# A two-layer graph network on one core: a re-planned instruction order, PSUM banks named by the planner, and layer norms' reciprocal roots on ScalarE

## The chip, the core and the metric

The kernel runs on one core of one Trainium2 chip. The metric is the device time in microseconds of one execution. Before the change it was 4487.69 us, the median of three runs (4481.99, 4487.69, 4490.15).

## The reference, cut to what matters

The input `x` is 16 batches of 1024 rows by 256 columns in fp32; `adj` is 16 matrices of 1024 by 1024 int32, of which only "larger than zero" matters. Two layers follow each other for each batch by itself.

Layer 0 is graph attention with 8 heads of width 32, and is followed by a layer norm, a product, a second layer norm and a residual:

```
q, k, v = heads(x @ Wq), heads(x @ Wk), heads(x @ Wv)
e = q k^T;  e = where(e >= 0, e, 0.2 * e)
h = softmax(where(adj > 0, e, -9e15)) @ v
x1 = layernorm(concat(layernorm(h), x) @ Wffn.T) + x
```

Layer 1 runs two more attentions whose scores are only a sum of a row term and a column term, then two layer norms around a feed-forward net of width 1024:

```
gat(h): Wh = h @ W; e = leaky_relu(Wh @ a_left + (Wh @ a_right)^T)
        softmax(where(adj > 0, e, -9e15), over rows) @ Wh
h = layernorm(x1 + gat(gat(x1)))
out = layernorm(h + relu(h @ w_ff1 + b_ff1) @ w_ff2 + b_ff2)
```

A layer norm multiplies each row by rsqrt(var + 1e-5). With four layer norms to a batch this reciprocal root of a column of variances is wanted in 14 places a batch, 224 in all.

## The kernel before, in words

**Engines.** TensorE does all products and transposes. For one head and one block of 128 keys (a "step", 1024 of them in all) TensorE makes 128x1024 scores (L601, tile `ps_s`), ScalarE multiplies them by 0.2 (L619), VectorE takes the larger of the two (L621), ScalarE takes the exponential (L624), GpSimd multiplies by the mask (L628), and TensorE multiplies by the values (L650, tile `ps_a`, two halves of the array at once with 33 or 64 columns each). The rest of a batch goes through tiles of one PSUM bank called `ps_m`: transposes of `x` (L355) and of the mask (L422), projections of q and k (L475, their high and low halves taken out in L478 on ScalarE and L480 on VectorE) and of v (L507), the head outputs (L677), the product with Wffn (L753, L756), layer 1's products (L785, L876, L901), and the feed-forward net (L941, L969, with L929 adding the residual). Each such tile is emptied by ScalarE or VectorE. The weights of layer 1's attention are made by VectorE alone (`attend`, L838 and L841).

**The order is written out by a planner.** All work is in Python generators ("threads"). Before anything is issued, a thread says `yield on(ENGINE=cost)`; it takes buffers by `yield take(pool)`, gives them back by `yield give(pool)`, and waits for events of other threads. The class `Order` keeps a clock for each engine and steps from one operation to the next: among those that could begin within 300 ns (`WINDOW`) of the earliest one it takes the one with the smallest due time (`aim`). The order in which the planner releases the threads is the program's order on each engine's queue; on the chip each engine works through its queue in that order and waits by semaphores. So the costs given to `on` and the constants `HOP` (added after each operation before another engine may go on) have no effect on what is computed. They set the order alone. Due times come from two tables of shares of a batch's slot of 253 us: `EARLY` for the first two batches, `AIM` for all the others and for the paces of the first, second and last batch (`fast0`, `fast1`, `fast15`).

**Buffers.** PSUM has 8 banks: two `scores` tiles of two banks each, one `acc` bank for the values, and three `misc` banks. `misc()` asks a pool with `bufs=3` for a tile, and the framework picks one of the three; the planner's own pool only counts them. `p` has five buffers.

**Around the change.** From the second batch on, `all_scores` takes both score buffers and issues the scores of two steps at once (`n = 2`). `all_values` waits for two steps (`GV = 2`) and issues both as one operation of the planner, cost `240 + 860 * GV`, and gives both `p` buffers back after it. `stats` computes mean and variance on VectorE (L333, L335), and then on GpSimd adds epsilon (L338) and raises to the power -0.5 (L340); `normalized` (L349) and the feed-forward's end (L982) wait for it. The GpSimd queue holds the 1024 mask products L628, and these 448 small instructions between them.

Batches overlap: while the scores of batch b are made, the rest of batch b-1 and the projections of batch b+1 fill TensorE's queue.

Of the kernel before, what the change touches and what calls it, by code (L numbers as in the profile page):

```python
# [18 lines left out]
EPS = 1e-5  # L19
# [15 lines left out]
class Order:  # L35
# [5 lines left out]

    HOP = dict(PE=100.0, ACT=70.0, DVE=60.0, POOL=70.0, SP=60.0)
    WINDOW = 300.0

# [3 lines left out]
    def __init__(self, **pools):  # L54
        self.clock = defaultdict(float)
        self.port = 0.0
        self.transfers = 0.0
        self.stretch, self.done, self.half = 0, 0.0, True
        self.pools = {k: [0.0] * n for k, n in pools.items()}
        self.queues = defaultdict(list)  # L60
        self.events = {}
        self.waiting = defaultdict(list)
        self.active = []
        self.made = 0
        self.now = 0.0
        self.busy = defaultdict(float)

    def add(self, thread, aim, ready=0.0):
        self.made += 1
        self.step({"gen": thread, "aim": aim, "no": self.made, "ready": ready}, None)  # L70

    def step(self, th, sent):
        while True:
# [19 lines left out]
            elif what == "take":  # L93
# [3 lines left out]
                th["ready"] = max(th["ready"], self.pools[arg].pop(0))  # L97
            elif what == "give":
                queue = self.queues[arg]
                if queue:  # L100
                    other = min(queue, key=lambda o: (o["aim"], o["no"]))
                    queue.remove(other)
                    other["ready"] = max(other["ready"], th["ready"])
                    self.step(other, None)
                else:
                    self.pools[arg].append(th["ready"])
# [27 lines left out]
    def run(self):  # L134
        while self.active:
            could = []
            for th in self.active:
                costs, shared, delay = th["op"]
                best = None
                for engine, cost in costs.items():  # L140
                    ready = th["ready"]
                    if th.get("last", ())[:2] == (engine, ready):
                        ready -= self.HOP[engine]
                    t = max(self.clock[engine], ready)
                    if shared and engine in ("DVE", "POOL"):
                        t = max(t, self.port)
                    if best is None or t + cost < best[0] + best[2]:
                        best = t, engine, cost
                could.append((best, th))
            first = min(c[0][0] for c in could)  # L150
            (t, engine, cost), th = min((c for c in could if c[0][0] <= first + self.WINDOW),
                                        key=lambda c: (c[1]["aim"], c[1]["no"]))
            if th["op"][1] and engine in ("DVE", "POOL"):

                lead = 100.0 if engine == "DVE" else -100.0
                before = [c for c in could if c[1]["op"][1] and c[0][1] in ("DVE", "POOL")
                          and c[0][1] != engine and c[0][0] + lead < t]
                if before:
                    (t, engine, cost), th = min(before, key=lambda c: (c[1]["aim"], c[1]["no"]))
            costs, shared, delay = th["op"]  # L160
            self.active.remove(th)
            end = self.clock[engine] = self.end(engine, t, cost)
# [4 lines left out]
            th["ready"] = end + self.HOP[engine]  # L167
# [10 lines left out]
def on(shared=False, delay=0.0, **costs):  # L178
    return "on", (costs, shared, delay)
# [45 lines left out]
def unshifted_path(  # L225
# [28 lines left out]
    AIM = dict(mask0=0.759, x=0.818, x_step=0, mask=0.747, mask_step=0.0264, qk0=0.614, qk1=0.898,  # L254
               qk_step=0.0231, v0=0.832, v1=0.974, v_step=0.0591, rows=-0.244, rows_step=0.0408, first0=0.12,
               first1=0.252, graph0=-0.009, graph1=0.21, graph_step=0, second=0.355, second_step=0.0335,
               normed=0.78, normed_step=0.026, ff_wait=(None, 0, 1, 0), ff=(0.532, -0.011, 0.487, 0.497),
               ff_step=0.0386, fast0=0.425, fast1=0.938, fast15=0.832, lead=3.15)

    EARLY = dict(x=0.87, x_step=0.005, mask=0.747, mask_step=0.0296, qk0=0.692, qk1=0.909, qk_step=0.0345,  # L260
                 v0=0.774, v1=1.001, v_step=0.0568, rows=-0.139, rows_step=0.0071, first0=0.082, first1=-0.169,
                 graph0=-0.195, graph1=-0.027, graph_step=0, second=0.302, second_step=0.0335, normed=0.781,
                 normed_step=0.02, ff_wait=(None, 0, 1, 0), ff=(0.633, -0.001, 0.488, 0.497), ff_step=0.0386)
# [13 lines left out]
    def misc(dtype=FT):  # L277
        return psum.tile([P, HALF], dtype, tag="misc", name="ps_m", bufs=bufs["misc"])
# [9 lines left out]
    minus_half = const.tile([P, TPH], FT, name="minus_half")  # L288
    nc.gpsimd.memset(minus_half, -0.5)
# [25 lines left out]
    def evacuate(n):  # L315
        return on(DVE=140 + 1.06 * n, ACT=150 + 0.87 * n)

    def evacuate_by(n):

        return on(DVE=190 + 1.06 * n, ACT=250 + 0.87 * n)  # L320
# [5 lines left out]
    def stats(srcs):  # L326
# [3 lines left out]
        for i, src in enumerate(srcs):  # L330
            st = small.tile([P, 6], FT, name="st")
            yield on(DVE=420)
            nc.vector.bn_stats(st, src)  # L333
            yield on(DVE=185)
            nc.vector.bn_aggr(mv[:, i, :], st)  # L335
        rs = small.tile([P, n], FT, name=f"rs{n}")
        yield on(POOL=260)
        nc.gpsimd.tensor_scalar(rs, mv[:, :, 1], EPS, None, op0=OP.add)  # L338
        yield on(POOL=450 + 150 * n, shared=True)
        nc.gpsimd.tensor_tensor(rs, rs, minus_half[:, :n], op=OP.pow)  # L340
        return mv, rs

    def normalized(dst, srcs, mv, rs):
        for i, (row, src) in enumerate(zip(dst, srcs)):
            if row is src:
                yield on(DVE=340, shared=True)
            else:
                yield on(DVE=440)
# [38 lines left out]
    def mask_part(b, t, halves):  # L387
# [22 lines left out]
        for i, ai in enumerate(ints):  # L410
            yield on(DVE=440, shared=True)
# [8 lines left out]
        yield on(PE=90 + 112 * n)  # L420
# [3 lines left out]
        yield on(ACT=150 + 225 * n)  # L424
# [19 lines left out]
    def x_pair(b, u):  # L444
# [7 lines left out]
        yield on(PE=450)  # L452
# [7 lines left out]
    def qk_part(b, g, o, nh):  # L460
# [12 lines left out]
        yield on(PE=1720)  # L473
# [3 lines left out]
        yield on(ACT=590)  # L477
        nc.scalar.copy(high.bitcast(FR), pa)  # L478
        yield on(DVE=690)
# [20 lines left out]
    def v_part(b, g, u):  # L500
# [3 lines left out]
        yield on(PE=1000)  # L504
# [15 lines left out]
    def project_v(b, g, t0):  # L520
# [3 lines left out]
        yield on(POOL=500)  # L524
# [5 lines left out]
    def warm_up():  # L530
# [3 lines left out]
        nc.scalar.copy(small.tile([P, TPH], FT, name="warm", bufs=1), minus_half)  # L534
# [46 lines left out]
    def all_scores():  # L581
        for b in range(B):
# [4 lines left out]
            for h in range(H):  # L587
                yield wait(("stack", b, h))
                q, kk = stacks[b, h]
                n = 2 if b else 1  # L590
                for t in range(0, NT, n):
                    due = t0 + (h * NT + t) / 2 * pace(b)
                    yield aim(due, AIM["lead"] * PACE)
                    for _ in range(n):
                        yield take("scores")
                    ps = [psum.tile([P, N], FT, tag="scores", name="ps_s") for _ in range(n)]
                    yield on(PE=450 * n)
                    for i in range(n):
                        for nh in range(NH):
                            cols = slice(nh * HALF, (nh + 1) * HALF)  # L600
                            nc.tensor.matmul(ps[i][:, cols], kk[:, (t + i) * P:(t + i + 1) * P], q[:, cols],  # L601
                                             start=True, stop=True)
                    if t + n == NT:
                        yield give("stacks")
                    for i in range(n):
                        yield start(weights(b, h, t + i, ps[i]), due + i * PACE / 2)

    def weights(b, h, t, ps):
# [3 lines left out]
        if b == 0:  # L612
            engine = yield on(ACT=1050, DVE=1230)
        else:
            engine = yield on(ACT=1050)
# [4 lines left out]
        yield on(DVE=1220)  # L620
        nc.vector.tensor_tensor(p, p, ps, op=OP.max)  # L621
        yield give("scores")
        yield on(ACT=1080)
# [3 lines left out]
        yield on(POOL=2050, shared=True)  # L627
# [3 lines left out]
    def all_values():  # L631
        for b in range(B):
            for h in range(H):
# [6 lines left out]
                for d in range(0, NT, GV):  # L640
                    for t in range(d, d + GV):
                        yield wait(("p", b, h, t))
                    yield aim(begin[b] + (h * NT + d + 2) / 2 * pace(b), SLOT)
                    yield on(PE=240 + 860 * GV)
                    for t in range(d, d + GV):
                        p = probs.pop((b, h, t))
                        for nh in range(NH):

                            m = VW if t else 64
# [796 lines left out]
```

## Time and profile before

| what | us |
|---|---|
| runs | 4481.99, 4487.69, 4490.15 |
| span of the profiled execution, first to last instruction | 4479.9 |
| TensorE busy with matmuls | 4325.9 (97%) |
| VectorE busy | 3311.9 (74%) |
| ScalarE busy | 2887.7 (64%) |
| GpSimd busy | 2474.9 (55%) |
| mean granted TensorE clock | 0.990 |

The profile gives a span for the profiled execution and no other time of it; the three runs lie 2.1 to 10.2 us above that span, the median 7.8 us. An engine's idle time says what it waited for last. TensorE's matmuls are pipelined, so a short wait can hide under the draining end of the matmul before it and then counts as busy; distances from one start to the next show it.

### The profile page before, as it was taken

The numbers are of one execution on the slowest core, as the hardware profiler recorded it, in microseconds if no ns is written. First come the engines' busy times: TensorE is split into PE (matmuls) and PEld (weight loads), VectorE is DVE, ScalarE is ACT, GpSimd is POOL, SyncE is SP. The second block draws the span as 40 slices with busy tenths as digits, with TensorE's granted clock in tenths as the row PEclk, the third lists the DMA queues.
The fourth block names the chain that finished last, engine by engine and source line by source line (L and its number), as shares of the span: only waits on it lengthen the run. The fifth ranks groups of instructions, "written<-read, shape, count | busy, mean of one in ns | idle before, by whom it ended". The sixth has DMA issues, their size and how long they took to land.

```text
span 4479.9 us, 57088 instructions
## 1 busy us (share of the span) xinstructions
PE 4325.9 (97%) x20299; PEld 2866.3 (64%) x20299; DVE 3311.9 (74%) x5263; ACT 2887.7 (64%) x4015; POOL 2474.9 (55%) x1544
## 2 busy tenths in 40 slices
PE   8888999999999999999999999999999999999998
PEld 3444656667666675766667666676666667666587
DVE  6877867687776877778777776877778777776754
ACT  6666675666667666666666666666666666666631
POOL 5756565554565556556554565546556554665610
PEclk9989999999999999999999999999999999999999
DMA  6423222232232313223231232323223231232100
GB/s 187 114 66 87 66 73 77 73 92 73 68 88 63 107 59 86 76 59 99 64 106 55 74 96 62 103 63 80 80 64 99 64 102 55 71 92 55 27 22 20
DMA packets 156209, 343.57 MB, mean 77 GB/s; under 512 B 21751, under 2 KB 24333, under 8 KB 155917
## 3 DMA queue, kind: packets, MB, share of 16 engines
q1 hardware_dynamic: 112140, 260.13, 20.8%
q10 hardware_dynamic: 43776, 79.71, 6.1%
q8 instruction: 164, 2.69, 0.3%
q14 instruction: 129, 1.05, 0.1%
HBM read 239.09 MB, written 100.66 MB: 76 GB/s over the span
## 4 chain that ended last, share of the span: by engine, by line
PE 69%; DVE 18%; issue 5%; POOL 5%; ACT 2%; DMA 0%; POOLq 0%; ACTq 0%; DVEq 0%
PE ps_a L650 16%; PE ps_s L601 9%; PE ps_m L901 8%; PE ps_m L876 8%; PE ps_m L941 7%; PE ps_m L969 6%; DVE att L841 5%; DVE att L838 5%; POOL p L628 4%; DVE p L621 4%; PE ps_m L785 3%; PE ps_m L475 3%; PE ps_m L753 2%; PE ps_m L756 2%; PE ps_m L355 2%
## 5 line engine op out<-in xcount | busy, mean ns | idle before, releaser
L628 POOL TENSOR_TENSOR p<-p,mask 128x1024 f32<-128x1024 f32 x1024 | 2232.2, 2197 | 1564.6 <-ACT p L624 1444.7
L621 DVE TENSOR_TENSOR p<-p,ps_s 128x1024 f32<-128x1024 f32 x1024 | 1211.1, 1214 | 399.3 <-ACT p L619 397.8
L624 ACT ACTIVATE p<-p 128x1024 f32<-128x1024 f32 x1024 | 1080.9, 1058 | 377.5 <-DVE p L621 355.7
L619 ACT ACTIVATE p<-ps_s 128x1024 f32<-128x1024 f32 x995 | 974.9, 1025 | 186.7 <-PE ps_s L601 172.1
L650 PE MATMUL ps_a<-p,v 128*33 128x512 f32 (+1 forms) x4096 | 1000.6, 606 | 24.2 <-POOL p L628 22.9
L601 PE MATMUL ps_s<-qs,ks 128*128 128x512 f32 x2048 | 634.5, 428 | 39.2 <-DVE p L621 38.3
L601 PEld LDWEIGHTS ps_s<-qs,ks 128*128 128x128 f32 x2048 | 349.5, 190 | 343.2 <-DVE p L621 106.2
L650 PEld LDWEIGHTS ps_a<-p,v 128*33 128x33 f32 (+1 forms) x4096 | 199.7, 114 | 531.3 <-issue 405.3
L901 PE MATMUL ps_m<-y,att 128*128 128x256 f32 x2048 | 480.5, 380 | 12.7 <-ACT v L516 11.0
L941 PE MATMUL ps_m<-rT,wf 128*128 128x256 f32 x2048 | 479.8, 384 | 10.7 <-ACT z L313 3.6
L969 PE MATMUL ps_m<-wf,hid 128*128 128x256 f32 x2048 | 475.1, 381 | 10.6 <-ACT xT L313 8.9
L876 PE MATMUL ps_m<-y,att 128*128 128x258 f32 x2048 | 472.4, 381 | 0.0
L969 PEld LDWEIGHTS ps_m<-wf,hid 128*128 128x128 f32 x2048 | 379.4, 190 | 78.6 <-issue 14.8
L876 PEld LDWEIGHTS ps_m<-y,att 128*128 128x128 f32 x2048 | 385.2, 189 | 63.6 <-issue 3.3
L901 PEld LDWEIGHTS ps_m<-y,att 128*128 128x128 f32 x2048 | 375.0, 189 | 77.3 <-ACT v L516 13.1
L941 PEld LDWEIGHTS ps_m<-rT,wf 128*128 128x128 f32 x2048 | 380.9, 192 | 63.4 <-ACT z L313 3.8
L838 DVE SCALAR_TENSOR_TENSOR att<-first,second 128x1024 f32<-128x1024 f32 x256 | 354.4, 1384 | 73.2 <-ACT first L825 73.2
L841 DVE SCALAR_TENSOR_TENSOR att<-mask,att 128x1024 f32<-128x1024 fp8e4 x256 | 352.0, 1375 | 8.7
L846 ACT ACTIVATE y<-y,check 128x258 f32<-128x258 f32 x256 | 130.9, 511 | 305.3 <-DVE check L844 278.4
L338 POOL TENSOR_SCALAR rs<-mv 128x2 f32<-128x2 f32 (+1 forms) x224 | 60.0, 268 | 410.9 <-DVE mv L335 410.8
L412 DVE TENSOR_SCALAR adj_b<-adj_i 128x512 fp8e4<-128x512 int32 x256 | 234.0, 958 | 14.8 <-DMA adj_i<-in_adj_dram 9.3
L950 ACT ACTIVATE hid<-ps_m,columns 128x256 f32<-128x256 f32 x372 | 159.2, 472 | 119.8 <-PE ps_m L941 94.3
(105 smaller groups left out, 4232.5 us busy)
## 6 DMA issues: line engine op xcount, KB each, us to landing
qs<-qk_halves SPq DMA_DIRECT2D x256, 256.0 KB, 4.2
ks<-qk_halves SPq DMA_DIRECT2D x256, 256.0 KB, 5.1
adj_i<-in_adj_dram ACTq DMA_DIRECT2D x240, 256.0 KB, 3.5
qk_halves<-high SPq DMA_DIRECT2D x128, 256.0 KB, 2.4
qk_halves<-low SPq DMA_DIRECT2D x128, 256.0 KB, 3.6
xr<-in_x_dram ACTq DMA_DIRECT2D x64, 256.0 KB, 3.1
x_kept<-x SPq DMA_DIRECT2D x64, 256.0 KB, 4.8
x<-x_kept SPq DMA_DIRECT2D x64, 256.0 KB, 6.8
```

The lines of the kernel that those rows point to most:

```text
L601: nc.tensor.matmul(ps[i][:, cols], kk[:, (t + i) * P:(t + i + 1) * P], q[:, cols], start=True, stop=True)
L619: nc.scalar.activation(p, ps, AF.Copy, scale=ALPHA)
L621: nc.vector.tensor_tensor(p, p, ps, op=OP.max)
L624: nc.scalar.activation(p, p, AF.Exp)
L628: nc.gpsimd.tensor_tensor(p, p, mask_of(b, t), op=OP.mult)
L650: nc.tensor.matmul(acc[nh * 64:nh * 64 + m, :], v[:, t, c:c + m], p[:, nh * HALF:(nh + 1) * HALF], start=(t == 0), stop=(t == NT - 1))
L838: nc.vector.scalar_tensor_tensor(e, first[:, 0, :], second[:, j:j + 1], first[:, 1, :], op0=OP.mult, op1=OP.max)
L841: nc.vector.scalar_tensor_tensor(e, mask_of(b, j), -1.0, e, op0=OP.mult, op1=OP.mult, accum_out=sums[:, j:j + 1])
L876: nc.tensor.matmul(pa[:, cols:cols + width], big[:, j, i * P:(i + 1) * P], rows[:, j, :width], start=(j == 0), stop=(j == NT - 1))
L901: nc.tensor.matmul(pa[:, i * D:(i + 1) * D], big[:, j, t * P:(t + 1) * P], y2[:, j, :D], start=(j == 0), stop=False)
L941: nc.tensor.matmul(pa[:, i * 2 * P:(i + 1) * 2 * P], wf1[:, dc, hc * P:(hc + 1) * P], rT[:, dc, :], start=(dc == 0), stop=(dc == DC - 1))
L969: nc.tensor.matmul(pa[:, i * D:(i + 1) * D], hid[hc // 2][:, hc % 2, i * P:(i + 1) * P], wf2[:, hc, :], start=(hc == 0), stop=False)
```

## The change

Nothing that is computed differs but the way to the reciprocal root. The change has five parts.

1. **Planner's costs.** `HOP` is split in a time before an operation (`HOP`) and one after it (`TAIL`); nearly all costs of `on` are given anew, most of them lower (for instance 910 for 1050 at L619, 962 for 1080 at L624, 1130 for 1220 at L621, while scores go from 450 to 471). A change on TensorE between the narrow value products and anything else costs the planner 93 ns (`SWITCH`). The choice between VectorE and GpSimd on their shared port goes by who asked first.
2. **Due times.** 33 of the entries of `AIM` and `EARLY` have other values.
3. **Grain.** The scores go one step at a time for every batch. The values go one step at a time too: the first of a pair still waits for both, the second has a due time at the start of its batch, and each gives its `p` buffer back by itself.
4. **Banks.** The planner remembers which slot of a pool a thread was given, and `misc()` asks for the bank of that slot by name.
5. **Reciprocal root.** `rs = exp(-0.5 * ln(var + eps))`, two activations on ScalarE in place of an addition and a power on GpSimd; the activation tables of logarithm and exponential are loaded at the start as one set.

```diff
-    HOP = dict(PE=100.0, ACT=70.0, DVE=60.0, POOL=70.0, SP=60.0)
+    HOP = dict(PE=53.0, ACT=35.0, DVE=36.0, POOL=80.0, SP=60.0)
+    TAIL = dict(PE=163.0, ACT=103.0, DVE=84.0, POOL=42.0, SP=0.0)
+    SWITCH = 93.0
...
+    def taken(self, th, pool, ready, slot):
+        th["ready"] = max(th["ready"], ready)
+        th["held"][pool].append(slot)
+        self.slot[pool] = slot
...
+            if engine == "PE":
+                if narrow != self.narrow:
+                    cost += self.SWITCH
+                self.narrow = narrow
...
-    AIM = dict(mask0=0.759, x=0.818, x_step=0, mask=0.747, mask_step=0.0264, qk0=0.614, qk1=0.898,
-               qk_step=0.0231, v0=0.832, v1=0.974, v_step=0.0591, rows=-0.244, rows_step=0.0408, first0=0.12,
-               first1=0.252, graph0=-0.009, graph1=0.21, graph_step=0, second=0.355, second_step=0.0335,
-               normed=0.78, normed_step=0.026, ff_wait=(None, 0, 1, 0), ff=(0.532, -0.011, 0.487, 0.497),
-               ff_step=0.0386, fast0=0.425, fast1=0.938, fast15=0.832, lead=3.15)
+    AIM = dict(mask0=0.759, x=0.7439, x_step=0.0012, mask=0.7438, mask_step=0.0264, qk0=0.6094, qk1=0.7723,
+               qk_step=0.0231, v0=0.863, v1=0.974, v_step=0.0591, rows=-0.2501, rows_step=0.0338, first0=0.1095,
+               first1=0.2264, graph0=-0.0093, graph1=0.2519, graph_step=0.0015, second=0.3518, second_step=0.0595,
+               normed=0.78, normed_step=0.058, ff_wait=(None, 0, 1, 0), ff=(0.5154, -0.0752, 0.487, 0.497),
+               ff_step=0.0581, fast0=0.4431, fast1=0.9245, fast15=0.8679, lead=1.9386)
...
     def misc(dtype=FT):
-        return psum.tile([P, HALF], dtype, tag="misc", name="ps_m", bufs=bufs["misc"])
+        return psum.tile([P, HALF], dtype, tag=f"misc{work.slot['misc']}", name="ps_m", bufs=1)
...
         rs = small.tile([P, n], FT, name=f"rs{n}")
-        yield on(POOL=260)
-        nc.gpsimd.tensor_scalar(rs, mv[:, :, 1], EPS, None, op0=OP.add)
-        yield on(POOL=450 + 150 * n, shared=True)
-        nc.gpsimd.tensor_tensor(rs, rs, minus_half[:, :n], op=OP.pow)
+        yield on(ACT=98)
+        nc.scalar.activation(rs, mv[:, :, 1], AF.Ln, bias=eps)
+        yield on(ACT=98)
+        nc.scalar.activation(rs, rs, AF.Exp, scale=-0.5)
...
-        nc.scalar.copy(small.tile([P, TPH], FT, name="warm", bufs=1), minus_half)
+        nc.scalar.preload_act_table_set("natural_log_exp_and_others")
...
-                n = 2 if b else 1
-                for t in range(0, NT, n):
+                for t in range(NT):
                     due = t0 + (h * NT + t) / 2 * pace(b)
                     yield aim(due, AIM["lead"] * PACE)
-                    for _ in range(n):
-                        yield take("scores")
...
-                for d in range(0, NT, GV):
-                    for t in range(d, d + GV):
-                        yield wait(("p", b, h, t))
-                    yield aim(begin[b] + (h * NT + d + 2) / 2 * pace(b), SLOT)
-                    yield on(PE=240 + 860 * GV)
+                for t in range(NT):
+                    yield wait(("p", b, h, t))
+                    if t % GV == 0:
+                        for other in range(t + 1, t + GV):
+                            yield wait(("p", b, h, other))
+                        yield aim(begin[b] + (h * NT + t + 2) / 2 * pace(b), SLOT)
+                    else:
+                        yield aim(begin[b], BIG)
+                    yield on(PE=860, narrow=True)
```

`EARLY` changes in the same manner (among others `mask` 0.747 to 0.681, `qk1` 0.909 to 0.9441, `first0` 0.082 to 0.1365, `first1` -0.169 to -0.0311). The other lines of the diff only put new costs in place of old ones.

## The prediction

> **What bounds the kernel now.** First the page: TensorE is busy 97% of the span, the next engine 74%. An average hides stages, so I next read the starts of `ps_s` in the trace: the scores of the 16 batches begin at 36.3, 203.7, 472.4, 752.2, 1024.3, then every 270.1 us (within 0.2) up to 3995.8. So there is a start of three batches, a steady state, and an end. The windows view over these stretches (busy us and instructions of each engine, granted clock, DMA share, GB/s):
>
> ```profile
> core 0: us, PE busy (x) PEld busy (x) DVE busy (x) ACT busy (x) POOL busy (x), PEclk, DMA share, GB/s
> 1834.80:2104.90 270.10, 266.27 (x1267) 177.75 (x1265) 204.11 (x325) 182.40 (x253) 152.72 (x97) 1.00 0.28 79
> 0.00:203.70 203.70, 171.82 (x702) 75.16 (x702) 156.90 (x168) 130.51 (x171) 136.97 (x78) 0.92 0.57 166
> 203.70:472.40 268.70, 238.13 (x1054) 142.48 (x1053) 194.73 (x289) 170.53 (x226) 162.24 (x88) 0.93 0.26 73
> 472.40:752.20 279.80, 265.94 (x1236) 174.60 (x1235) 202.22 (x326) 176.02 (x241) 164.64 (x95) 0.98 0.28 77
> 4261.80:4480.00 218.20, 205.27 (x1004) 177.53 (x1002) 110.23 (x281) 55.16 (x122) 20.36 (x40) 0.99 0.06 22
> ```
>
> The steady period is TensorE's: 98.6% busy, while ScalarE stands at 68% and GpSimd at 57%. Idle time is 3.8 us a period. It is more at both ends: 31.9, 30.6 and 13.9 us in the first three stretches, where the clock is also granted at 0.92 to 0.98, and 12.9 us in the last.
>
> Busy is not the floor, since waits hide under draining matmuls. From start-to-start distances I put each matmul at what it takes back to back (216 ns for 128x256, 235 for scores, 430 for a pair of value matmuls on both halves, and so on). A batch's matmuls come to 255 us. A pair of value steps takes 1842 ns from its first start to what follows, 122 over 4 x 430, and the matmuls before it take some 94 over theirs: 216 ns for each run of values, x 32 = 6.9 us. Of 270.1 - 255 - 6.9 = 8.2 us, about 6 are real waits (3.8 idle, some 2 hidden) and the rest is spent going into and out of scores. So **6 us a period is all that an order can win there**. Which waits they are, from the waits view of TensorE for 1540 to 4060 us (total, times, longest):
>
> ```profile
> PE ps_m L901 <- ACT v L516: 9.0, 9, 1.0
> PE ps_a L650 <- POOL p L628: 7.1, 11, 0.8
> PE ps_m L969 <- ACT xT L313: 6.5, 9, 0.7
> PE ps_m L507 <- ACT v L516: 4.7, 9, 0.5
> PE ps_m L677 <- ACT ho L313: 4.1, 9, 0.5
> ```
>
> Nine times in nine periods: waits for `ps_m` banks or evacuations at fixed places of the plan, not chance. The timeline shows the first of them:
>
> ```profile
> 2011.69 1.88 PE L475 MATMUL ps_m<-xT,wk 128*128 128x512 f32 x4
> 2015.00 1.16 PE L507 MATMUL ps_m<-wv,xT 128*128 128x128 f32 x8 [0.54 <-ACT v L516]
> 2016.74 0.36 ACT L516 ACTIVATE v<-ps_m 128x256 f32<-128x256 f32 x1
> 2017.16 1.99 PE L901 MATMUL ps_m<-y,att 128*128 128x256 f32 x8 [1.00 <-ACT v L516]
> ```
>
> L475's bank is not free until L480 on VectorE has read it, which is queued behind a run of L838/L841; the other banks are emptied by L516, and TensorE waits for it twice.
>
> **What the Trainium skill says.** "ScalarE: Activation LUTs", section "Table sets: the hidden batching unit": logarithm and exponential are both in `natural_log_exp_and_others`, so one load serves both; cheap functions are in every set. The trace before has one ACT_TABLE_LOAD, 1283 ns; no run here shows two functions yet. "SBUF — State Buffer", section "SBUF: two separate sides": a GpSimd operation and a VectorE one with two SBUF inputs take their shared port pair exclusively. That agrees with L841, which averages 1375 ns and takes 1.22 in undisturbed places. "TensorE: Matmul & The Clock Gate", section "What's actually happening": the array's clock is halved when TensorE was idle of late. Here the clock is below 1.00 only in stretches with idle time, as above.
>
> **The change part by part.**
>
> *Reciprocal root.* The lines of the groups view (count, busy us, mean ns, idle before):
>
> ```profile
> L628 POOL TENSOR_TENSOR p<-p,mask 128x1024 f32<-128x1024 f32 x1024 | 2232.2, 2197 | 1564.6 <-ACT p L624 1444.7 <-issue 72.6 <-PE ps_m L941 11.7
> L338 POOL TENSOR_SCALAR rs<-mv 128x2 f32<-128x2 f32 (+1 forms) x224 | 60.0, 268 | 410.9 <-DVE mv L335 410.8
> L340 POOL TENSOR_TENSOR rs<-rs,minus_half 128x2 f32<-128x2 f32 (+1 forms) x224 | 177.0, 790 | 18.3
> L859 ACT ACTIVATE second<-check 128x8 f32<-128x8 f32 x32 | 6.5, 203 | 0.8 <-DVE check L886 0.5 <-DVE check L790 0.4
> ```
>
> Removed: 60.0 + 177.0 = 237 us of GpSimd, 14.8 a period (152.7 to 137.9). Added: 448 activations. The exponential is bounded by L859, 203 ns; the logarithm has a pointer for its bias, about 280 ns by the skill's section "What ACT_TABLE_LOAD costs" (estimate). So 0.48 us x 14 = 6.8 a period, ScalarE 182.4 to 189.2 of 270 (70%). Direct worth: nothing. L628 has 1564.6 us of idle time before it, and a mask product that stood behind L338/L340 was held by 47 us in all 1024 (worked out from its start against the end of its exponential); in the steady state values begin a median 2.8 us after their mask product ends. That slack covers it. At the end 1.06 us of root becomes about 0.5 twice: 1 us. The wait for VectorE's variances, 410.8 us on GpSimd, moves to ScalarE. Behind it then stand L619, L624 and every evacuation of `ps_m`, for which TensorE waits. Bounds: 14 waits of 0 to 0.5 us, at most 7 a period if TensorE felt each; I take none, because the planner now books that place in ScalarE's queue.
>
> *Banks.* Were the framework turning its three banks in strict order, a name from the plan would win much. It isn't; the timeline has three L507 tiles and an L677 tile filled while L969's tile is still open (L929 ends it):
>
> ```profile
> 1836.01 1.89 PE L969 MATMUL ps_m<-wf,hid 128*128 128x256 f32 x8
> 1840.71 0.50 PE L677 MATMUL ps_m<-ident,ho 97*128 97x97 f32 x4
> 1842.80 2.84 PE L507 MATMUL ps_m<-wv,xT 128*128 128x128 f32 x24
> 1847.44 0.44 PE L929 MATMUL ps_m<-ident,rT 128*128 128x128 f32 x2
> ```
>
> Between nothing and the 2 us a period of bank waits above; I take 0.4.
>
> *Costs, due times.* Old L619 cost 1050 + 70 = 1120 ns before VectorE may go on, against 1025 measured; new occupancy 910, with 35 and 103 around it, 1048. L621 was 1220 + 60, against 1214 measured. The old plan believed both engines 5 to 9% slower than they are, and so placed evacuations where they are not. `second_step`, `normed_step` and `ff_step` go up by half or more: the products L876, L901, L941 are spread over the slot. I take 2 of the remaining 5.6 us.
>
> *Grain.* Scores: going in costs TensorE about 60 ns less and coming out 90 more, so 32 more runs are about 1 us a period at most; a score no longer waits for both buffers (values then scores: some 1.4 us a period over the plain 122 ns), I take -0.2 net. Values: nothing if pairs stay together, as the second one's early due time asks.
>
> *Moved DMAs* (adj and x on ScalarE's queue, the rest on SP's): DMA share 0.28, TensorE's longest wait for one is 4.4 us, for x at the start. Nothing.
>
> Sum: (0.4 + 2 + 0.2) = 2.6 us x 14 periods = 36. The start has 76 us idle, some 20 of it before the first matmul, and some 40 us lost to the half clock; the plan for its first two batches has its own table. I take 15. End 2. So 4479.9 - 53 = 4427 for a span, and 7.8 more for the median: **4435**.
>
> **Rivals.** *All of it* (15%): the truer costs take nearly 5 us x 14 = 70, 40 of the start's waits and clock, 8 of the end: 118, giving 4370. For it: waits that repeat to 0.1 us are waits that a plan can know. Against: 98.6% busy leaves little. *The waits move* (20%): other evacuations come late at other places, and ScalarE queues behind variances where GpSimd did: 4460 to 4497, say 4475. For it: the 410.8 us that GpSimd stood waiting for variances fall to some other queue. *Slower* (15%), by one mechanism: pairs of values are cut. Once the mates are scheduled apart, operations with due times ahead of the batch's start (`rows` has -0.25 of a slot) may come between them. Each cut costs 216 ns of TensorE; against a gain of 53 it decides from 245 cuts on, about half of the 512 pairs. With 400 cut and the other gain at 60%, +86 - 32: 4540. Against: only some 24 operations of TensorE a batch have such due times, and the planner charges itself 93 ns for a switch but doesn't avoid it. *It does not do what it says*: were the table set reloaded at each logarithm, 224 x 1.3 = 290 us on ScalarE; the skill's one set speaks against it; under 1%, within the slower 15%.
>
> **How the numbers follow.** The likeliest case has 50%, its own range 4408 to 4462. Measurement tells 0.2%, 9 us, from no change. Faster: 50 + 15 + 11 of the 20 = 76%. Same: 7%. Slower: 2 + 15 = 17%. Low end: within the good rival, 4368. High end: the moved waits and the beginning of the slower case, 4505; about 1 in 10 lies outside on each side.
>
> **What would show it.** Right: a period of 267 to 268 us between starts of `ps_s`; TensorE idle under 3 us a period; GpSimd down by some 237 us, ScalarE up by 90 to 110 less what its other work changes; one table load; eight value matmuls still standing together. Wrong: a period of 270 or more, value runs of four, new waits of TensorE for ScalarE where ScalarE itself waited for variances, or a period under 265.

## The result and the profile after

The changed kernel takes 4463.08 us (median of four runs, 4461.74 to 4464.54), against 4485.99 us of the kernel before in the same comparison. The ratio is 0.9949, with a 95% interval of 0.9936 to 0.9962. It is faster, by 0.5% where 1.2% was forecast: 23 us in place of 52. The time lies inside the stated range; the gain is less than half the forecast.

The spans of the two profiled executions are 4461.6 and 4479.9 us, so they show 18.3 us of it. (Every run with a span on record lies 1.7 to 2.1 us above it; so the profiled execution before was probably the quickest of its three, 4481.99 us, and most of the 7.8 us that the forecast adds to its span is the difference between executions.) The windows view of the profile after, cut at the starts of the batches' scores as before (columns: busy us and instructions of each engine, granted clock, DMA share, GB/s):

```profile
core 0: us, PE busy (x) PEld busy (x) DVE busy (x) ACT busy (x) POOL busy (x), PEclk, DMA share, GB/s
0.00:191.20 191.20, 160.67 (x689) 72.04 (x689) 137.38 (x161) 133.33 (x173) 133.85 (x76) 0.97 0.59 172
191.20:457.40 266.20, 231.80 (x1032) 137.59 (x1033) 188.65 (x292) 169.84 (x236) 148.22 (x69) 0.92 0.26 72
457.40:727.70 270.30, 263.28 (x1234) 172.72 (x1233) 202.40 (x326) 184.50 (x271) 147.39 (x69) 0.99 0.27 77
727.70:3985.70 3258.00, 3219.69 (x15152) 2128.89 (x15149) 2379.30 (x3935) 2240.69 (x3325) 1728.36 (x819) 1.00 0.27 78
3985.70:4461.60 475.90, 460.10 (x2201) 347.79 (x2198) 296.00 (x580) 245.67 (x431) 142.56 (x66) 0.99 0.11 33
```

The same view of the kernel before, from the fourth batch's scores on:

```profile
752.20:3995.80 3243.60, 3193.55 (x15152) 2129.79 (x15150) 2454.58 (x3906) 2186.35 (x3030) 1832.34 (x1153) 1.00 0.28 78
3995.80:4480.00 484.20, 456.50 (x2164) 344.22 (x2162) 303.45 (x574) 224.26 (x348) 178.75 (x134) 0.99 0.11 30
```

The first three batches end at 727.7 in place of 752.2 us: 24.5 us won. The last stretch, from the scores of batch 15 on, takes 475.9 in place of 484.2: 8.3 won. But the twelve periods between, where 2.6 us each, 31 us, were forecast, take 3258.0 in place of 3243.6: **14.4 us lost**. A period is 271.5 us on average and no longer regular (267.5 to 273.7), where it was 270.1 or 270.2 in all but the first of the twelve (272.1).

The waits view of TensorE for the steady part, 998 to 3715 us (total, times, longest):

```profile
PE ps_s L604 <- DVE p L622: 14.6, 13, 2.2
PE ps_m L972 <- ACT xT L319: 4.4, 5, 1.1
PE ps_m L428 <- DVE rT L378: 2.3, 4, 0.8
PE ps_m L361 <- ACT hid L953: 1.7, 1, 1.7
```

Of the five fixed waits of the old plan that the prediction shows, once or more in each period, four are gone; L972's for `xT` (formerly L969's) is left, five times. Scores now wait for their buffer (L604 for L622's maximum, formerly L601 for L621), which they hardly did in the old steady state. TensorE's idle time in the twelve periods fell only from 50.1 to 38.3 us (3243.6 - 3193.55, 3258.0 - 3219.69), and its busy time rose by 26 us for the same matmuls. Two stretches of 3.4 us in these periods, at 1344.8 and 3246.0 us, are granted half the clock, and can make up at most 3.4 us of it. The rest I put down to waits too short to show as idle and to the other order of the matmuls; which of them, isn't shown.

The groups of the reciprocal root and of the mask product, in the columns of the groups view:

```profile
L629 POOL TENSOR_TENSOR p<-p,mask 128x1024 f32<-128x1024 f32 x1024 | 2287.7, 2253 | 1883.4 <-ACT p L625 1391.9 <-ACT mask L432 358.3 <-PE ps_a L654 53.1
L344 ACT ACTIVATE rs<-mv,eps 128x2 f32<-128x2 f32 (+1 forms) x224 | 66.3, 296 | 102.2 <-DVE mv L341 98.2 <-DMA adj_i<-in_adj_dram 1.6
L346 ACT ACTIVATE rs<-rs 128x2 f32<-128x2 f32 (+1 forms) x224 | 45.7, 204 | 6.8
L540 ACT ACT_TABLE_LOAD x1 | 1.3, 1283 | 2.6 <-issue 2.6
```

This part came out as priced: 296 and 204 ns against 280 and 203, one table load. ScalarE's wait for variances is 98.2 us where GpSimd's was 410.8.

### The profile page after: what moved, and what is told of

It is laid out like the page before. It is cut to its first block, busy times and chain, and to the rows that moved or that the text cites. A ratio compares the mean times of both kernels' runs of the same rounds, so it can differ in the third digit from the quotient of the medians.

```text
span 4461.6 us, 56826 instructions
## 1 busy us (share of the span) xinstructions
PE 4335.5 (97%) x20299; PEld 2859.0 (64%) x20299; DVE 3203.7 (72%) x5292; ACT 2974.0 (67%) x4433; POOL 2300.4 (52%) x1096
## 4 chain that ended last, share of the span: by engine, by line
PE 86%; DVE 9%; ACT 3%; issue 1%; DMA 1%; POOL 0%; SPq 0%; ACTq 0%; DVEq 0%; POOLq 0%
PE ps_a L654 18%; PE ps_s L604 11%; PE ps_m L879 10%; PE ps_m L904 10%; PE ps_m L944 9%; PE ps_m L972 9%; PE ps_m L481 4%; DVE p L622 3%; PE ps_m L788 3%; PE ps_m L756 3%; PE ps_m L759 2%; PE ps_m L513 2%; PE ps_m L361 2%; DVE att L841 2%; DVE att L844 2%; PE ps_m L932 1%
## 5 line engine op out<-in xcount | busy, mean ns | idle before, releaser
L629 POOL TENSOR_TENSOR p<-p,mask 128x1024 f32<-128x1024 f32 x1024 | 2287.7, 2253 | 1883.4 <-ACT p L625 1391.9
L622 DVE TENSOR_TENSOR p<-p,ps_s 128x1024 f32<-128x1024 f32 x1024 | 1219.5, 1214 | 467.7 <-ACT p L620 464.5
L620 ACT ACTIVATE p<-ps_s 128x1024 f32<-128x1024 f32 x1000 | 991.1, 1021 | 164.4 <-PE ps_s L604 127.4
L604 PE MATMUL ps_s<-qs,ks 128*128 128x512 f32 x2048 | 685.2, 440 | 57.2 <-DVE p L622 54.5
L604 PEld LDWEIGHTS ps_s<-qs,ks 128*128 128x128 f32 x2048 | 339.8, 190 | 382.0 <-DVE p L622 150.6
L972 PE MATMUL ps_m<-wf,hid 128*128 128x256 f32 x2048 | 479.6, 384 | 8.5 <-ACT xT L319 5.2
L972 PEld LDWEIGHTS ps_m<-wf,hid 128*128 128x128 f32 x2048 | 384.2, 192 | 67.3 <-ACT xT L319 6.6
L841 DVE SCALAR_TENSOR_TENSOR att<-first,second 128x1024 f32<-128x1024 f32 x256 | 392.8, 1534 | 26.4 <-ACT first L828 26.2
L339 DVE BATCH_NORM_STATS2 st<-y 128x6 f32<-128x256 f32 x256 | 104.9, 410 | 150.8 <-ACT y L319 149.8
L319 ACT COPY y<-ps_m 128x512 f32<-128x512 f32 x105 | 61.6, 586 | 188.4 <-PE ps_m L932 104.2
```

Source lines behind the costliest of these rows:

```text
L604: nc.tensor.matmul(ps[:, cols], kk[:, t * P:(t + 1) * P], q[:, cols], start=True, stop=True)
L620: nc.scalar.activation(p, ps, AF.Copy, scale=ALPHA)
L629: nc.gpsimd.tensor_tensor(p, p, mask_of(b, t), op=OP.mult)
L841: nc.vector.scalar_tensor_tensor(e, first[:, 0, :], second[:, j:j + 1], first[:, 1, :], op0=OP.mult, op1=OP.max)
L972: nc.tensor.matmul(pa[:, i * D:(i + 1) * D], hid[hc // 2][:, hc % 2, i * P:(i + 1) * P], wf2[:, hc, :], start=(hc == 0), stop=False)
```

## The experiments

The planner's answer to a change of its inputs is a whole new order, so I kept apart two kinds of run. In the five marked "same order", and in the last (search_1_named, in the order of search_1), every engine gets its instructions in the order of the kernel named, but for what is said (in banks_newest one neighbouring pair on VectorE also changes places). In the others the order is planned anew.

### Banks and root, each by itself in a fixed order

*no_banks*, same order as the changed kernel, the framework chooses the bank again:

```diff
     def misc(dtype=FT):
-        return psum.tile([P, HALF], dtype, tag=f"misc{work.slot['misc']}", name="ps_m", bufs=1)
+        return psum.tile([P, HALF], dtype, tag="misc", name="ps_m", bufs=bufs["misc"])
```

> The changed kernel with the framework choosing among the three misc banks again; the planned order is the same on every engine. Theory A (the order alone makes the difference, banks and root are worth nothing): 4457 to 4469 us, like the changed kernel's 4463. Rival B (naming the banks gave some of the gain): 4475 us or more.

Measured 4435.92 us, ratio to the kernel before 0.9889 (0.9873 to 0.9906). Both expectations missed, and in the direction that neither had: without the named banks the changed kernel is 27 us faster. In the same window as above (998 to 3715 us) its scores wait less for their buffer:

```profile
PE ps_s L604 <- DVE p L622: 5.8, 12, 1.6
```

Since the order is the same, the two traces can be compared matmul by matmul, from start to start. Of the 27 us, 16 arise in front of the first write of 338 `ps_m` tiles which the plan's name puts into a bank at most 12 instructions after its last read, where the framework had left more than 12. Another 6 arise in front of scores, and the rest is spread over the other products.

*banks_in_before*, the mirror image: same order as the kernel before, the planner's slots remembered (`taken`, `held` and `slot` as in the change) and `misc()` naming the bank:

```diff
-                th["ready"] = max(th["ready"], self.pools[arg].pop(0))
+                self.taken(th, arg, *self.pools[arg].pop(0))
...
-        return psum.tile([P, HALF], dtype, tag="misc", name="ps_m", bufs=bufs["misc"])
+        return psum.tile([P, HALF], dtype, tag=f"misc{work.slot['misc']}", name="ps_m", bufs=1)
```

> The kernel before in its own order with only the banks named by the planner's slots. Theory A: 4478 to 4493 us. Rival B: 4475 us or less.

Measured 4562.29 us, ratio 1.0173 (1.0157 to 1.0190), outside both expectations again: 77 us slower for this edit alone, the order unchanged.

Its waits view of TensorE shows whose banks came late:

```profile
PE ps_m L684 <- DVE check L893: 51.1, 12, 4.6
PE ps_m L684 <- DVE low L487: 21.8, 13, 3.5
```

The edit adds lines, so numbers are higher by 7: L684 is the transpose of a head's output (L677 in the kernel before), L883 a layer-1 product (L876), and L893 the small copy by VectorE (L886) that is the last to read this product's tile. The timeline of one of these twelve:

```profile
1952.34 3.65 PE L883 MATMUL ps_m<-y,att 128*128 128x258 f32 x16
1962.48 0.49 DVE L989 SCALAR_TENSOR_TENSOR z<-z,rs,bl 128x256 f32<-128x256 f32 x1
1962.88 0.15 DVE L893 COPY check<-ps_m 128x2 f32<-128x2 f32 x1
1963.18 0.88 PE L684 MATMUL ps_m<-ident,ho 97*128 97x97 f32 x4 [4.23 <-DVE check L893]
1963.85 2.41 PE L883 MATMUL ps_m<-y,att 128*128 128x258 f32 x5
```

And the same place of the kernel before, some 29 us earlier on its clock:

```profile
1934.16 0.55 PE L677 MATMUL ps_m<-ident,ho 97*128 97x97 f32 x4 [0.46 <-ACT ho L313]
1934.55 3.68 PE L876 MATMUL ps_m<-y,att 128*128 128x258 f32 x16
1937.65 0.15 DVE L886 COPY check<-ps_m 128x2 f32<-128x2 f32 x1
```

There the transpose and the next layer-1 product both start 3 us before L886 has read the earlier product's tile: two other banks were free, and the framework used them. The planner's name gave the transpose the one bank that was still being read, because the threads of the next two products had taken the other two before their turn on TensorE came. Both stood empty through the whole wait: the last reads of their earlier tiles ended at 1945.8 us (L487) and 1952.2 us (L320).

The wait is not the whole price. The windows view of this run, over the twelve periods and over a stretch about this wait:

```profile
753.70:4071.50 3317.80, 3215.16 (x15152) 2151.56 (x15150) 2454.52 (x3906) 2189.67 (x3030) 1831.16 (x1153) 0.99 0.27 77
1961.00:1967.80 6.80, 4.62 (x14) 3.80 (x15) 4.89 (x7) 1.99 (x3) 1.90 (x2) 0.50 0.10 39
```

The twelve periods take 74 us more than in the kernel before: TensorE's idle time is 53 us more, and its busy time 22 us more for the same matmuls. The granted clock shows where the latter comes from. It is halved beside each of the twelve long waits (4.2 to 4.6 us), for 3.4 us at the first and 6.8 or 6.9 us at the others, and nowhere else in these periods; the eleven waits of 1.6 us for L487 have no such stretch. Five of L883's matmuls behind the wait take 2.41 us (0.48 each), where the sixteen of the product ahead of it take 3.65 (0.23 each).

The bad choice is not particular to this place. I counted in the programs. Of 1558 tiles for which all three banks had been used, the framework puts 1549 (order of the changed kernel; 1539 in that of the kernel before) into the bank whose last read lies furthest back, seen from the tile's first write. The planner's names do so for 1013 and 960. In program order, about two of three banks are free at a first write. So the tiles written within four instructions of the last read of their bank go from 85 to 187 in the changed order, and from 52 to 134 in the old one.

*banks_newest* tries whether it is the choice or the naming. Same order as the changed kernel, named banks, but labels exchanged so that the bank freed last is handed out:

```diff
-                self.taken(th, arg, *self.pools[arg].pop(0))
+                free = self.pools[arg]
+                ready, slot = free.pop(0)
+                if free:
+                    free[-1], slot = (free[-1][0], slot), free[-1][1]
+                self.taken(th, arg, ready, slot)
```

> The changed kernel, same order on every engine, but where the planner has several free banks it hands out the name of the one freed last instead of the one freed first. Counted in the program, 220 of the 1561 misc tiles are then first written within four instructions of the last read of their bank, against 187 in the changed kernel and 85 with the framework choosing. Theory D (a name bound when a thread takes the bank, before its turn on TensorE, turns banks round too soon, and this costs 27 us in the changed kernel): slower than the changed kernel's 4463, about 4465 to 4485 us. Rival E (it is the naming as such, one tag for each bank and its waits, whichever bank is picked): 4457 to 4466 us.

Measured 4468.04 us (4467.73 to 4469.76), ratio 0.9963 (0.9949 to 0.9977). It is the side of the choice (theory D), but 5 us from the changed kernel, with intervals of the ratios that overlap, so this run alone wouldn't settle it. What speaks for the choice is the matmuls' comparison with no_banks and the timeline above, where two banks stood empty.

*root_gpsimd*, same order as the changed kernel, addition and power issued on GpSimd where the planner books ScalarE:

```diff
         yield on(ACT=98)
-        nc.scalar.activation(rs, mv[:, :, 1], AF.Ln, bias=eps)
+        nc.gpsimd.tensor_scalar(rs, mv[:, :, 1], EPS, None, op0=OP.add)
         yield on(ACT=98)
-        nc.scalar.activation(rs, rs, AF.Exp, scale=-0.5)
+        nc.gpsimd.tensor_tensor(rs, rs, minus_half[:, :n], op=OP.pow)
```

> The changed kernel's order, but at the two places of the reciprocal root GpSimd's addition and power are issued in place of the two activations; the planner still books ScalarE for them. Theory A: 4457 to 4469 us. Rival C (the logarithms waiting in ScalarE's queue are what ate the gain, some 1.5 us of 14 periods or more): 4440 us or less. If taking the power off GpSimd was itself the gain: 4475 us or more.

Measured 4497.96 us, ratio 1.0031 (1.0020 to 1.0041): 35 us slower than the changed kernel. So the logarithms in ScalarE's queue did not eat the gain: with GpSimd's operations in their place the kernel is slower (rival C falls). By the expectation, 4475 us or more would say that taking the power off GpSimd was itself the gain; the next run denies that for the old order. In its waits view, GpSimd stands waiting for the variances in front of the addition L344:

```profile
POOL rs L344 <- DVE mv L341: 955.2, 174, 50.7
```

The same wait of ScalarE in the changed kernel was 98.2 us. Matmul by matmul against the changed kernel's trace, 13.5 of the 31 us of difference between the spans arise in front of L361's transposes of the normed rows `y`.

*root_in_before*, same order as the kernel before, with the two activations, and the table load at the start:

```diff
         yield on(POOL=260)
-        nc.gpsimd.tensor_scalar(rs, mv[:, :, 1], EPS, None, op0=OP.add)
+        nc.scalar.activation(rs, mv[:, :, 1], AF.Ln, bias=eps)
         yield on(POOL=450 + 150 * n, shared=True)
-        nc.gpsimd.tensor_tensor(rs, rs, minus_half[:, :n], op=OP.pow)
+        nc.scalar.activation(rs, rs, AF.Exp, scale=-0.5)
```

> The kernel before in its own order with only the reciprocal root as logarithm and exponential on ScalarE, tables loaded as one set. Theory A: 4478 to 4493 us, like the kernel before. Rival C: 4505 us or more. If the root was the gain: 4470 us or less.

Measured 4485.60 us, ratio 1.0002 (0.9993 to 1.0010). The root by itself is worth nothing where the order was planned for GpSimd. What root_gpsimd shows is the price of the wrong queue in an order that was planned for the other one.

### The order, planned anew

no_banks and root_in_before leave one account for the rest. From 4485.3 to 4435.9 us, 49 us, is due to the order with its costs, due times and grain. This order is planned for a root on ScalarE; whether one as good can be planned for a root on GpSimd was not tried. How much of that is the costs, how much the particular order? Three runs, all with the framework choosing the banks. nudge_a and nudge_b each change one cost by about a thousandth:

```diff
-        yield on(DVE=1130)
+        yield on(DVE=1131)
```

```diff
-        yield on(POOL=2098, shared=True)
+        yield on(POOL=2100, shared=True)
```

> The changed kernel with the framework choosing the banks, and one cost of the planner, VectorE's maximum, 1131 ns in place of 1130. Nothing else differs, but the planner's order comes out otherwise and its own clock ends at 4441 us in place of 4387. Theory F (the due times were fitted to one outcome of a planner that answers to single nanoseconds, and the chip feels a part of it): 4455 to 4500 us against 4436. Rival G (the chip's time depends on the costs and due times, not on the particular outcome): 4430 to 4442 us.

Measured 4473.34 us, ratio 0.9973 (0.9963 to 0.9983).

> As nudge_a, but with GpSimd's mask product at 2100 ns in place of 2098; the planner's own clock ends at 4505 us. Theory F: 4480 to 4540 us, and slower than nudge_a. Rival G: 4430 to 4442 us.

Measured 4534.92 us, ratio 1.0107 (1.0090 to 1.0124). Theory F holds: one nanosecond more in one cost takes away 37 of the 49 us, two nanoseconds in another make the kernel slower than before by 1.1%.

*grain_back* has scores and values by two steps as before the change:

```diff
-                for t in range(NT):
+                n = 2 if b else 1
+                for t in range(0, NT, n):
...
-                    yield on(PE=471)
+                    yield on(PE=471 * n)
...
-                for t in range(NT):
-                    yield wait(("p", b, h, t))
+                for d in range(0, NT, GV):
+                    for t in range(d, d + GV):
+                        yield wait(("p", b, h, t))
...
-                    yield on(PE=860, narrow=True)
+                    yield on(PE=860 * GV, narrow=True)
```

> The changed kernel with the framework choosing the banks, and with scores by two steps from the second batch on and values by two steps as one operation, as before the change; costs, due times and root as changed. The planner's own clock ends at 4450 us. If the grain itself is worth what was predicted (0.2 us of 14 periods): within 10 us of what a plan of that end gives, so like nudge_a. If single scores are what makes the changed order fast: 4490 us or more. If they cost: 4430 us or less.

Measured 4463.02 us, ratio 0.9952 (0.9935 to 0.9968). It lies between the cases that were to be told apart: 10 us under nudge_a, and between no_banks (4436) and nudge_b (4535), which share its costs to a thousandth. What the grain is worth by itself stays open, since it cannot be changed without another order.

Then I looked for other due times: small random steps of the entries of `AIM` and `EARLY`, keeping what makes the planner's own clock end sooner. *search_1* and *search_2* are two of its results; *search_4* did the same with two of TensorE's costs raised. The core of the edits of search_1, and the costs of search_4:

```diff
-    AIM = dict(mask0=0.759, x=0.7439, ..., fast0=0.4431, fast1=0.9245, fast15=0.8679, lead=1.9386)
+    AIM = dict(mask0=0.8594, x=0.7302, ..., fast0=0.5147, fast1=0.9239, fast15=0.8762, lead=1.93)
```

```diff
-    SWITCH = 93.0
+    SWITCH = 108.0
...
-                    yield on(PE=471)
+                    yield on(PE=530)
```

> The changed kernel with the framework choosing the banks and with other due times, found by trying small steps of them and keeping those with which the planner's own clock ends sooner: 4368 us in place of 4387. Costs, grain and root as changed. Theory F: about 30 to 50 us over the planner's end, 4398 to 4420 us. Rival G (what the planner gains on its own clock is lost on the chip): 4430 us or more.

Measured 4422.46 us, ratio 0.9860 (0.9844 to 0.9876): the fastest of all, and again regular at 268.7 us a period. It lies 2.5 us above theory F's range, and 7.5 below rival G's.

> As search_1, another set of due times; the planner's own clock ends at 4377 us. Theory F: 4407 to 4428 us, slower than search_1. Rival G: 4430 us or more.

Measured 4437.85 us, ratio 0.9894 (0.9877 to 0.9910). It is slower than search_1 as forecast, but it falls into rival G's range: the gain of 10 us on the planner's clock against no_banks is not there on the chip.

> Due times found in the same way with two costs of TensorE put nearer to what the trace shows, 530 ns for a step of scores in place of 471 and 108 in place of 93 for a change between values and others; the planner's own clock, with these, ends at 4433 us. If those two costs are most of what the plan leaves out: 4425 to 4445 us and within 10 us of the plan. If the plan misses other things too: 4450 to 4480 us.

Measured 4464.96 us, ratio 0.9953 (0.9937 to 0.9970). The two raised costs are not most of what the plan leaves out.

> search_1 in the same order with the banks named by the planner as in the change: 200 tiles are written within four instructions of the last read of their bank, against 83. Theory D: 20 to 40 us slower than search_1. If the cost seen in the changed kernel was particular to its order: within 6 us of search_1.

Measured 4467.61 us, ratio 0.9964 (0.9950 to 0.9978), 45 us slower than search_1. The edit is that of banks_in_before's second hunk, in the order of search_1. In a third order the named banks cost again, 5 us more than theory D's range and more than in the changed kernel.

The planner's clock at its end beside the chip's median, framework's banks throughout:

| kernel | planner's end, us | chip, us | difference |
|---|---|---|---|
| search_1 | 4368 | 4422.5 | 54 |
| search_2 | 4377 | 4437.9 | 61 |
| no_banks | 4387 | 4435.9 | 49 |
| search_4 (other costs) | 4433 | 4465.0 | 32 |
| nudge_a | 4441 | 4473.3 | 32 |
| grain_back | 4450 | 4463.0 | 13 |
| before (other costs) | 4460 | 4485.3 | 25 |
| nudge_b | 4505 | 4534.9 | 30 |

Over a spread of 137 us in the plans the chip follows in the main. The three orders with the earliest ends on the changed kernel's costs lie 49 to 61 us over their plan, the other three on these costs 13 to 32. That is what one expects when an order is picked because its clock ended early, but with six orders it isn't shown. search_4 and the kernel before don't bear on it, since their costs, and with them their plan's end, are others. The kernel before and its plan agreed on the period to 0.1 us (270.1). The changed kernel's plan has 265.6 us a period on average over the twelve, and is itself irregular (261.1 to 270.9); the chip has 271.5, of which 2.0 are due to the banks (no_banks: 269.5).

## Why the prediction was wrong

**The step that failed is "Banks".** It read correctly that the framework does not turn its banks in strict order, and then bounded the edit "between nothing and the 2 us a period", taking 0.4 as a gain. A loss was left out. Measured in the changed order it is a loss of 27 us, 24 of them in the twelve periods (3258.0 against no_banks' 3233.7): 2.0 a period with the other sign. The same edit costs 77 us in the old order and 45 in search_1's. The timeline shown in that very step held a hint: where the framework already picks a bank that is free, a plan's name has little to win. Its loss was not to be read there; it takes the count above.

The measured time lies in the range of the rival "the waits move" (4460 to 4497). Half of that rival's account fits: other evacuations came late at other places. The half on ScalarE, that it would queue behind variances where GpSimd did, doesn't: its wait for them is 98.2 us, and the order is worth its 49 us with the root on ScalarE.

**The steps "Costs, due times" and "Grain", start and end** were together 48 us (2.2 x 14 + 15 + 2), and no_banks against before is 45.7 us between the profiled spans. The sum is right by luck; its terms aren't. The windows of no_banks:

```profile
458.50:728.10 269.60, 263.09 (x1234) 172.69 (x1233) 204.41 (x326) 185.27 (x271) 147.38 (x69) 0.99 0.27 77
728.10:3961.80 3233.70, 3208.90 (x15153) 2130.02 (x15149) 2383.07 (x3935) 2238.17 (x3325) 1732.59 (x819) 1.00 0.27 79
3961.80:4434.20 472.40, 458.18 (x2201) 346.90 (x2198) 294.70 (x580) 245.44 (x431) 142.73 (x66) 0.99 0.11 33
```

The start gave 24.1 us (752.2 - 728.1) where I took 15, the end 11.8 (484.2 - 472.4) where I took 2, and the steady part 9.9 (3243.6 - 3233.7), 0.8 a period where I took 2.2. In the steady part idle time did halve, from 50.1 to 24.8 us; 15 us of it came back as busy time of the same matmuls. The finer grain of the scores may have a part in that (501 runs of two steps and 16 of one became 333 and 346), but no run shows it by itself. The same shows in search_1. Its twelve periods:

```profile
724.30:3948.50 3224.20, 3213.96 (x15156) 2126.70 (x15154) 2343.05 (x3904) 2258.73 (x3358) 1729.41 (x819) 1.00 0.28 79
```

Only 10.2 us of idle time are left, 40 less than in the kernel before, and the periods are 19 us shorter. So idle time is not what an order can win, and the 6 us a period that the prediction allowed an order are not reached by any of these: search_1 wins 1.6.

**"Reciprocal root: direct worth nothing"** held in the order of the kernel before (ratio 1.0002). ScalarE is busy 86 us more (2974.0 - 2887.7), GpSimd 174.5 less, not 237, mostly since L629 takes 2253 ns on average where L628 took 2197.

**The range's mechanism for "slower"** was cut pairs of values. There are 58 runs of half a pair where there were none, and 534 runs of values where there were 512: 22 more, some 5 us at 216 ns (an estimate). It didn't decide; the loss came from a part I had booked as a gain. Of the signs named ahead, the period (271.5 us, not 267 to 268) and TensorE's idle time (38.3 / 12 = 3.2 us a period, not under 3) said wrong; the one table load and the pairs, of which 467 of 512 still stand alone as pairs, said right.

**"Waits that repeat to 0.1 us are waits that a plan can know"** is half true. A plan that knows them can be had (search_1), but an order found by fitting is not explained by the costs it was fitted with: a cost's change by 0.1% undoes most of it.

## What to carry to other kernels

Leave the choice of a buffer to whoever knows the order of first use; a name bound when a producer reserves the buffer, before its turn in the queue, turned buffers round too soon in three orders. The price showed as short waits scattered over the waits view in one, and as a long wait in each period, with half the clock behind it, in another. A plan's name bound at the tile's first write was not tried. When an order is made by a greedy planner, treat one outcome as one draw: perturb a cost by a thousandth before giving a cause to a gain. And bound an edit below nothing as well when it takes a decision away from something whose decisions the profile shows to be good.

## What the runs showed of the hardware that I had not expected

Little of the hardware itself. In banks_in_before a wait of 4.2 us on TensorE had 6.8 us of half clock beside it, eleven times in eleven after the first (which had 3.4 us), while waits of 1.6 us had none, eleven times in eleven. So a wait can cost more than its length.

In the kernel before, the first two matmuls of a run of scores start 335 ns apart (median of the steady part), and those after them 231 to 234, across the border between two steps too. I don't know why.

The mask product on GpSimd got slower on average, 2197 to 2253 ns, though 448 small instructions had left its queue and VectorE's busy time fell (3311.9 to 3203.7 us). Its median did not move (2141 and 2142 ns), so it is some of the products that take longer; whether overlaps with VectorE on the port of the prediction's page did that, I haven't tried.
